# Two attention layers, one core: output projection with tokens on partitions, softmax sums turned to columns through DRAM

## Chip, cores and metric

The kernel runs on one core of a Trainium2 chip, all in float32. The metric is the device time of one execution in microseconds, the median of the runs. The engines carry these names in the profile: PE is TensorE's matmul, PEld its weight load, DVE is VectorE, ACT is ScalarE, POOL is GpSimd, SP is SyncE, which issues the DMAs.

## What is computed

x has 8 images of 32x32 tokens with 256 channels, so 8 batches of N = 1024 tokens. Layer 0 is attention with 4 heads and a residual; layer 1 is attention with a 32-wide key, a gamma and a residual.

```python
# layer 0, per batch; C = 256, h = 4 heads
qkv = xf @ W_qkv                       # 1024 x (4 * 768)
atten = softmax(q k^T * C**-0.5)       # over keys, per head
res = concat_heads(atten @ v) @ W_out + b_out + xf
# layer 1, per batch
f, g, hh = x @ Wf + bf, x @ Wg + bg, x @ Wh + bh
y = gamma * (softmax(g f^T) @ hh) + x
```

## The kernel before

Everything is one pass over *steps*. A step is one head (or layer 1) of one batch and one block (blk) of 512 queries. For each batch the order is the four heads of layer 0, two blocks each, and then layer 1 of the batch before, two blocks; after the last batch its own layer 1 follows. In each step the loop at L801 collects lists of small tasks: the scores of this step, the block sums and the product p x of the step before (`one`), the division and projection of the step before that (`two`), and whatever prepares the next head or batch. Each list comes with a begin and an end between 0 and 1, and `weave` (L755) sorts all tasks by their place in it and issues them in that order. TensorE, VectorE and ScalarE then work through exactly this order[...] (a manual schedule, L771); the order on POOL and SP is left to a scheduler. So the numbers in the lists decide what stands between two dependent tasks.

The weights of a head are folded: W_q W_k^T for the scores and W_v W_out for the output, so a head multiplies p with x itself and then with the folded 256x256 matrix wvo. Large products use seven block products instead of eight (`seven`, L219). It makes three tasks, one, two and three, which collect in three PSUM banks x, y and z: after task one ScalarE copies bank x to e and VectorE adds bank y to it (u); after task two VectorE makes v = y + e and one output block; task three adds two further products into banks y and z, which VectorE must have read by then, and two more output blocks follow. Within one `seven` TensorE thus waits for VectorE between task two and task three, and for ScalarE's e between one and two, unless other work stands there. The six "ps" banks serve these and layer 1's scores; two "psm" banks serve transposes (px, pt), projections (po, pr_v, pm_fg) and the like.

A layer 0 step: `scores` runs two `seven` groups of tokens (g = 0 and 2), each followed by exponentials on ScalarE (L472, L473), which give p. `sums` (L490) makes four block sums s1 to s4 of p for the next `seven`, then the softmax sums: m, rs, and an all-reduce over partitions on POOL, which leaves the sum of every query on all partitions (rb, L524). `invert` (L530) takes a 512-wide reciprocal and stores one row to the tile `check`. `products` (L536) makes y = x^T p with one `seven`. One step later `divide` (L557) multiplies y, 128x1024, with the inverse sums, and `project` (L563) multiplies wvo with y (po, channels on partitions) and adds it into x1T, the transposed output of layer 0. `queries` (L425) makes the next head's q with another `seven`, and its block sums qs. `value_sums` and `key_sums` make block sums of x and of its transpose x0T (from `transpose_rows`, px).

A layer 1 step: `scores` (L649) makes eight 128x512 tiles ps_l, four at a time[...]; ScalarE copies each to s_l, VectorE takes maxima (L702, L706, L708: smax), POOL all-reduces them to cmax (L710), and VectorE subtracts (L717) before ScalarE's exponentials (L722). `values` gives v_l (pr_v), `row_products` (L728) multiplies with it (pa_l), divides by the sum and adds to the rows of x1. Those rows come from `turn_back` (L605), which transposes x1T back. At the end the inverse sums in `check` are tested against limits (L859 to L866); a general branch behind `tc.If` takes over if any lies outside, which these inputs don't do.

## Time and profile before

| what | us |
|---|---|
| median of 3 runs | 2469.9 (2469.7 to 2473.68) |
| the profiled execution's own time | 2468.4 |
| its span | 2466.5 |
| PE busy | 2394.2 |
| DVE busy | 1843.4 |
| ACT busy | 612.8 |
| POOL busy | 249.6 |
| 512-wide reciprocals (L532), 64 | 214.0 |
| divisions of y (L559), 64 | 77.9 |
| additions of po into x1T (L581, L586), 128 | 89.4 |
| all-reduces of the sums (L524), 64 | 213.2 |

A busy time is the time in which at least one instruction of that engine ran, and the span is that of one execution. Matmuls are pipelined, and the page models their ends, so a PE that is 97% busy isn't at its peak 97% of the time. Rows in the timeline read: start, length, engine, line, operation, output<-input, shape, how many, and in brackets how long the engine stood idle before, and what ended that. A row of float32 matmul counts two records for each matmul that the program issues.

### The profile page before, as it was taken

To read this page: it belongs to the slowest core of one execution; us is meant where nothing else is said; L and a number is where in the kernel's file an instruction comes from. 1 tells how busy PE (TensorE), PEld (TensorE's weight loads), DVE (VectorE), ACT (ScalarE), POOL (GpSimd) and SP (SyncE) were. 2 spreads that over 40 slices of the span, in tenths; PEclk is the share of its full clock that TensorE was granted. 3 is DMA by queue.
4 is the path that set the end of the run, shared out by engine and by line. 5 is a ranking of instruction groups with operands and counts; after the bars stand their busy time and mean duration, and the time that the engine had idled before them with its cause. 6 is when DMAs were issued, how large, how long until landed. Compare 5 with 4: busy or idle time off the path is not lost.

```text
span 2466.5 us, 24718 instructions
## 1 busy us (share of the span) xinstructions
PE 2394.2 (97%) x10096; PEld 1858.4 (75%) x10096; DVE 1843.4 (75%) x2398; ACT 612.8 (25%) x985; POOL 249.6 (10%) x93
## 2 busy tenths in 40 slices
PE   8999999999999999999999999999899999999997
PEld 6777777777777677776877768777687776877766
DVE  5778887785878768787687776777767777677764
ACT  2222222232222322223222232222322223222232
POOL 0111111110111101111011110111101111011110
PEclk9999999999999999999999999999999999999999
DMA  3000000000000000000000000000000000000000
GB/s 111 1 1 1 18 1 1 0 1 35 1 1 1 1 35 1 0 1 0 35 1 1 1 0 35 1 1 1 1 35 0 1 1 1 18 1 1 1 9 28
DMA packets 11786, 23.30 MB, mean 9 GB/s; under 512 B 4496, under 2 KB 6416, under 8 KB 11664
## 3 DMA queue, kind: packets, MB, share of 16 engines
q1 hardware_dynamic: 11664, 21.64, 2.5%
q8 instruction: 81, 1.33, 0.2%
q14 instruction: 41, 0.34, 0.0%
HBM read 13.11 MB, written 8.39 MB: 9 GB/s over the span
## 4 chain that ended last, share of the span: by engine, by line
PE 88%; DVE 10%; ACT 1%; issue 1%; DMA 0%; SPq 0%; POOL 0%; DVEq 0%; ACTq 0%
PE psy_y L232 13%; PE psy L232 13%; PE pa_l L735 9%; PE psz L232 9%; PE psz_y L232 9%; PE psx_y L232 9%; PE psx L232 8%; PE po L572 6%; PE psy_q L232 3%; DVE s L511 3%; PE psz_q L232 2%; PE psx_q L232 2%; PE pr_v_l L403 1%; PE ps_l L659 1%; PE pm_fg L383 1%; ACT s_l L668 1%
## 5 line engine op out<-in xcount | busy, mean ns | idle before, releaser
L524 POOL PARTITION_ALL_REDUCE rb<-rs x64 | 213.2, 3332 | 1532.6 <-DVE rs L522 1532.6
L472 ACT ACTIVATE p<-p 128x1024 f32<-128x1024 f32 x128 | 135.3, 1057 | 782.6 <-DVE p L249 782.6
L232 PE MATMUL psy<-qs,xs 128*128 128x256 f32 x1024 | 262.9, 379 | 1.7 <-DVE qs L443 1.7
L232 PE MATMUL psx<-q,x0T 128*128 128x256 f32 x1024 | 262.8, 379 | 0.0
L232 PE MATMUL psz<-q,xs 128*128 128x256 f32 x1024 | 262.8, 379 | 0.0
L572 PE MATMUL po<-y,wvo 128*128 128x512 f32 x512 | 246.3, 604 | 16.4 <-DVE x0T L167 13.0
L232 PE MATMUL psx_y<-p,x 128*128 128x256 f32 x1024 | 241.9, 379 | 0.0
L232 PE MATMUL psz_y<-ss,x 128*128 128x256 f32 x1024 | 241.9, 379 | 0.0
L232 PE MATMUL psy_y<-s,xt 128*128 128x256 f32 x1024 | 241.9, 379 | 0.0
L232 PEld LDWEIGHTS psx<-q,x0T 128*128 128x128 f32 x1024 | 194.2, 190 | 50.2 <-issue 26.8
L735 PE MATMUL pa_l<-v_l,s_l 128*128 128x257 f32 x1024 | 228.3, 380 | 0.1
L735 PEld LDWEIGHTS pa_l<-v_l,s_l 128*128 128x128 f32 x1024 | 194.3, 190 | 32.2 <-issue 3.9
L232 PEld LDWEIGHTS psy<-qs,xs 128*128 128x128 f32 x1024 | 194.5, 190 | 28.5 <-DVE qs L443 2.1
L232 PEld LDWEIGHTS psz<-q,xs 128*128 128x128 f32 x1024 | 194.6, 190 | 26.5
L232 PEld LDWEIGHTS psy_y<-s,xt 128*128 128x128 f32 x1024 | 194.6, 190 | 26.5
L232 PEld LDWEIGHTS psz_y<-ss,x 128*128 128x128 f32 x1024 | 194.6, 190 | 26.5
L232 PEld LDWEIGHTS psx_y<-p,x 128*128 128x128 f32 x1024 | 194.6, 190 | 26.5
L532 DVE RECIPROCAL rb<-rb 128x512 f32<-128x512 f32 x64 | 214.0, 3343 | 0.0
L572 PEld LDWEIGHTS po<-y,wvo 128*128 128x128 f32 x512 | 97.0, 192 | 107.1 <-issue 75.9
L249 DVE TENSOR_TENSOR u<-psy,e 128x512 f32<-128x512 f32 x128 | 88.5, 691 | 105.5 <-PE psy L232 95.8
L261 ACT ACTIVATE p<-psx 128x512 f32<-128x512 f32 x128 | 76.5, 597 | 282.9 <-PE psx L232 282.7
L232 PE MATMUL psy<-qs,x0T 128*128 128x256 f32 x512 | 133.9, 384 | 5.5 <-DVE v L249 5.5
(112 smaller groups left out, 3063.3 us busy)
## 6 DMA issues: line engine op xcount, KB each, us to landing
out_dram<-x SPq DMA_DIRECT2D x15, 512.0 KB, 2.6
x<-in_x_dram SPq DMA_DIRECT2D x14, 512.0 KB, 4.4
w<-in_L_conv_W_qkv_dram SPq DMA_DIRECT2D x4, 768.0 KB, 9.1
x<-in_x_dram SPq DMA_DIRECT2D x4, 256.0 KB, 4.0
w<-in_L_conv_W_out_dram SPq DMA_DIRECT2D x4, 256.0 KB, 9.3
check<-rb SPq DMA_DIRECT2D x64, 2.0 KB, 1.6
out_dram<-x SPq DMA_DIRECT2D x4, 128.0 KB, 1.8
wh_sb<-in_L_conv_Wh_dram SPq DMA_DIRECT2D x1, 256.0 KB, 2.7
```

Of the source, the lines that this page charges most:

```text
L232: nc.tensor.matmul(banks[k][:, ts(i, w)], lhsT=lhsT, rhs=rhs, start=first and n == 0, stop=True, skip_group_check=True,)
L249: nc.vector.tensor_tensor(dst, shaped(banks[k]), shaped(other), ALU.add)
L261: copy(outs["11"](), shaped(banks["x"]))
L383: nc.tensor.matmul(pm[:m], lhsT=w()[:, c, d * P : d * P + m], rhs=src()[:, c, ts(k, NB)], start=(c == 0), stop=(c == CC - 1),)
L403: nc.tensor.matmul(pm[:, ts(j, C)], lhsT=src()[:, c, ts(2 * t2 + j, P)], rhs=w()[:, c, :], start=(c == 0), stop=(c == CC - 1),)
L472: exp(both, both)
L511: made["l"][i]()
L524: nc.gpsimd.partition_all_reduce(t, r.rearrange("p e i -> p (e i)"), P, bass_isa.ReduceOp.add)
L532: nc.vector.reciprocal(r, r)
L572: nc.tensor.matmul(pm, lhsT=folded[self.h][1][:, c, ts(e, P)], rhs=self.y[blk][:, c, :], start=(c == 0), stop=(c == CC - 1),)
L659: nc.tensor.matmul(pm, lhsT=self.f[ts(r, CK), ts(j0 + r, P)], rhs=self.g[ts(r, CK), ts(blk, NB)], start=True, stop=True,)
L735: nc.tensor.matmul(pm[:, : C + 1], lhsT=p[:, j, ts(ti, P)], rhs=v[:, j, : C + 1], start=(j == 0), stop=(j == NT - 1),)
```

## The change

The projection changes sides: y is now the stationary operand, so po has tokens on partitions, and its rows are added straight to the rows of x1. The inverse sum of a query is then one number per partition, and VectorE scales and adds in one operation. To bring the sums from a row to columns, the first row of rb is stored to DRAM and loaded back as a 128x4 tile, and the reciprocal is taken of that tile. Division, x1T's additions and `turn_back` go; x1's rows begin as x + b_out (`residual`), and x1T is made by `transpose_rows` in block 0 of the next batch's head 3. All copies of transposes are on ScalarE. The lists move: block sums s1, s2 at 0.08 to 0.32 of a step, s3, s4 at 0.4 to 0.7, the softmax sums at 0.7 to 0.95, po at 0.4 to 0.8. The test of the inverse sums moves ahead of the last row products. Several pools change size.

```diff
+    bout_sb = const.tile([P, C], F32, tag="bout", name="bout_sb")
+    inverse = const.tile([P, B * HEADS * NBLK * HT], F32, tag="inverse", name="inverse")
...
     def transpose_rows(b, src, dst, layer):
...
-            copy_on(c, dst[b][:, c, ts(k, NB)], pt)
+            nc.scalar.copy(dst[b][:, c, ts(k, NB)], pt)
...
+    def residual(b):
+        def piece(i):
+            if i == 0:
+                rows1[b] = tile_of("rows", [P, NT, C], f"x1_{b}")
+            nc.vector.tensor_tensor(
+                rows1[b][:, ts(i, 2), :], rows[b][:, ts(i, 2), :],
+                bout_sb.unsqueeze(1).broadcast_to([P, 2, C]), ALU.add,
+            )
+        return [partial(piece, i) for i in range(NT // 2)]
...
                 nc.gpsimd.partition_all_reduce(
                     t, r.rearrange("p e i -> p (e i)"), P, bass_isa.ReduceOp.add
                 )
-            return [partial(piece, i) for i in range(4)] + [first, second]
+                line = tile_of("line", [1, NB], f"line_{n}")
+                nc.sync.dma_start(line, t[0:1, :])
+                self.r[blk] = st = tile_of("st", [P, HT], f"st_{n}")
+                with nc.allow_non_contiguous_dma(reason="a row of sums turns into columns"):
+                    nc.sync.dma_start(st, line.rearrange("o (t p) -> p (o t)", p=P))
+            return [partial(piece, i) for i in range(4)], [first, second]
...
         def invert(self, blk):
-            r = self.r[blk]
-            nc.vector.reciprocal(r, r)
-            k = (self.b * HEADS + self.h) * NBLK + blk
-            nc.sync.dma_start(check[k : k + 1, :], r[0:1, :])
+            n = self.first + blk * HT
+            nc.vector.reciprocal(inverse[:, n : n + HT], self.r[blk])
...
-        def divide(self, blk):
...
         def project(self, blk):
+            def task(t2):
+                pm = tile_of("psm", [P, NB], f"po_{self.name}_{blk}_{t2}")
+                for j in range(2):
+                    for c in range(CC):
+                        nc.tensor.matmul(
+                            pm[:, ts(j, C)],
+                            lhsT=self.y[blk][:, c, ts(2 * t2 + j, P)],
+                            rhs=folded[self.h][1][:, c, :],
+                            start=(c == 0),
+                            stop=(c == CC - 1),
+                        )
+                for j in range(2):
+                    ti = 2 * t2 + j
+                    n = self.first + blk * HT + ti
+                    acc = rows1[b][:, blk * HT + ti, :]
+                    nc.vector.scalar_tensor_tensor(
+                        acc, pm[:, ts(j, C)], inverse[:, n : n + 1], acc, ALU.mult, ALU.add
+                    )
...
-        def turn_back(self):
...
-        s=2, rows=2, xT=3, v=2, q=2, qs=2, xt=1, ss=1, s2=1, s3=1, m0=1, m1=1, rs=1, rb=2,
-        y=1, e=2, u=2, w=2, eh=2, uh=2, wh=2, r=8, ps=6, psm=2,
+        s=2, rows=4, xT=2, v=2, q=2, qs=2, xt=1, ss=1, s2=1, s3=1, m0=1, rs=1, rb=1,
+        y=2, e=2, u=2, w=1, eh=1, uh=1, st=2, r=8, line=4, ps=6, psm=2,
...
-            if a.h == 1 and blk == 0 and a.b + 1 < B:
+            if a.h == 2 and blk == 0 and a.b + 1 < B:
                 load_x(a.b + 1)
+            if a.h == 0 and blk == 1:
+                lists.append((residual(a.b), 0.3, 1))
...
-            lists.append((u.sums(k), 0.08, 0.4))
-            lists.append(([partial(u.invert, k)], 0.6, 0.7))
-            lists.append((u.products(k), 0.42, 1.0))
+            sums, keys = u.sums(k)
+            lists.append((sums[:2], 0.08, 0.32))
+            lists.append((sums[2:], 0.4, 0.7))
+            lists.append((keys, 0.7, 0.95))
+            lists.append((u.products(k), 0.4, 1.0))
...
-            lists.append(([partial(u.divide, k)], 0, 0.04))
-            lists.append((u.project(k), 0.05, 0.4))
+            lists.append(([partial(u.invert, k)], 0.34, 0.36))
+            lists.append((u.project(k), 0.4, 0.8))
...
-        if change and blk == 1 and a.b > 0:
-            lists.append((nxt[0].queries(), 0.05, 0.4))
+        if change and a.b > 0:
+            if blk == 0:
+                lists.append((transpose_rows(a.b - 1, rows1, x1T_of, 1), 0.02, 0.4))
+            else:
+                lists.append((nxt[0].queries(), 0.05, 0.4))
...
-        if not l0 and blk == 1:
-            lists.append((a.turn_back(), 0, 0.25))
-            if nxt is None:
-                lists.append((final.queries(), 0.45, 1))
+        if nxt is None:
+            lists.append((transpose_rows(B - 1, rows1, x1T_of, 1), 0.82, 0.9))
+            lists.append((final.queries(), 0.9, 1))
...
-    run(own[:1], s0[:1], prod[:1], s0[1:], own[1:2], prod[1:2])
-    weave((own[2:] + prod[2:] + back, 0, 1), (s1, 0, 1), (p0, 0, 1))
-    weave((final.products(0), 0, 1), (p1, 0, 1))
+    run(own[:1], s0[:1], prod[:1], s0[1:], prod[1:2])
+    weave((prod[2:] + own[1:], 0, 1), (s1, 0.3, 0.9), (p0, 0.1, 1))
+    weave((final.products(0), 0, 1), (p1, 0, 0.9), ([judge, decide], 0.9, 1))
```

## The prediction

> **What bounds the kernel now.** I read first the page's busy times and its chain of work that ended last, then the busy times by stretch, then the timeline of single stretches, and beside them the order in which the changed kernel's instructions stand on each engine.

> ```profile
> PE 2394.2 (97%) x10096; PEld 1858.4 (75%) x10096; DVE 1843.4 (75%) x2398; ACT 612.8 (25%) x985; POOL 249.6 (10%) x93
> ...
> PE 88%; DVE 10%; ACT 1%; issue 1%; DMA 0%; SPq 0%; POOL 0%; DVEq 0%; ACTq 0%
> ```

> TensorE sets the end. A 256-column matmul record starts every 0.2155 us when nothing holds it (64 of 257 columns took 13.87 us in the chain, 0.217 each). With that price for every record I come to about 2351 us of work and some 115 us in which TensorE stands or runs slowly: about 18 in the first 60 us, 25 in the last 130, the rest at places that repeat in each batch. VectorE matters only where TensorE waits for it.

> ```profile
> 1121.00:1154.00 33.00, 29.56 (x131) 21.43 (x130) 28.59 (x34) 10.29 (x17) 6.82 (x2) 0.95 0.00 1
> 1154.00:1185.00 31.00, 30.00 (x118) 18.97 (x117) 18.74 (x26) 10.80 (x18) 1.78 (x1) 0.94 0.00 1
> ...
> 1246.00:1307.00 61.00, 60.73 (x252) 47.52 (x251) 48.30 (x60) 12.49 (x23) 6.47 (x2) 1.00 0.00 1
> ```

> Columns: stretch, length, PE, PEld, DVE, ACT, POOL, granted clock. The first two are the two layer 1 steps of a batch, the third two layer 0 steps. Layer 0 has nearly no gap (0.3 in 61 us), layer 1 has several us, and there the clock falls too. So removing VectorE work from layer 0 can save next to nothing; what counts is what stands between two dependent TensorE groups.

> [...]

> **The change, part by part.**

> Vector work. Removed per layer 0 step: the 512-wide reciprocal (L532, 3.343 us), the division (L559, 1.217), two additions x1T<-po (L586, 2 x 0.683): 5.93. Added: four 128x256 multiply-adds from PSUM at 0.484 (row L745), a 4-wide reciprocal at about 0.17 (row L743): 2.11. Eight times, four residual pieces of 0.69. Over 64 steps 244 us less and 22 more. The cover is total: this time lies beside TensorE, so I book it at nothing; if it were on the path it would be most of 222.

> TensorE. po: 8 records of 512 columns become 16 of 256, the same columns; weight loads take 190 ns under 215. The transposes of x1 are as many as before (128 records). Zero. They move from the second layer 1 step to head 3, block 0: +2.1 us there, -2.1 there.

> DMAs. One row store to check (1.6) becomes a row store and a column load of 512 elements, both on SP's queue, behind the all-reduce (3.3). The column load is not in the trace: not below zero, as it replaces nothing; at least 1.6, and at most 9 (the 256-element bout_sb load landed after 9.2, behind weights). I take 2.5. The sums end about 0.5 us before the next step starts, so columns stand about 7.5 us into it; VectorE's reciprocal comes at 7 to 8 there, its next consumer for TensorE some 4 us later. Nothing for 1.6 to 6; 9 would cost about 2 us in 24 steps. Queued behind that reciprocal on VectorE are two additions into p and the third block sum; behind the row store on SP's queue stand the column load, x loads and stores of out, none needed within 10 us. On POOL the all-reduce moves to the step's end, ahead of the next maximum's; rb has one buffer now, free once the row has landed, 10 us before that maximum. All at nothing, with that cover; without it each us late counts once per step.

> *Layer 0, the lost spacer.* This is the main item. A scores group is three tasks; the third overwrites a bank that VectorE must first read (tile v). Before, po stood between:

> ```profile
> 1250.26 1.03 PE L232 MATMUL psy<-qs,xs 128*128 128x256 f32 x4
> ...
> 1251.12 1.88 PE L572 MATMUL po<-y,wvo 128*128 128x512 f32 x4
> ...
> 1253.27 1.13 PE L232 MATMUL psy<-qs,x0T 128*128 128x256 f32 x4 [0.27 <-DVE v L249]
> ```

> po is moved to 0.4-0.8 of the step, so in block 0 of heads 1 and 2 the first group runs one, two, three with nothing between. The trace has that case at the start:

> ```profile
> 21.23 1.02 PE L232 MATMUL psy_q<-xs,wt 128*128 128x512 f32 x2
> ...
> 22.29 0.69 DVE L249 TENSOR_TENSOR v_q<-psy_q,e_q 128x512 f32<-128x512 f32 x1 [1.81 <-PE psy_q L232]
> ...
> 23.04 1.13 PE L232 MATMUL psy_q<-x0T,wt 128*128 128x512 f32 x2 [0.78 <-DVE v_q L249]
> ```

> 1.81 us from start to start, less 0.86 of work: 0.95, with 0.1 of restart 1.05.

> Second, the block sums' last adds go to 0.7-0.95. In a step with the next head's query sums, VectorE then has, after v (ready 5.0 us before the step's end): v 0.72, p 0.61, m 1.14, qs 0.61, rs 0.72 and 0.35, qs 0.61, two y at 0.38: 5.5 us, before the last two adds into p. Those come 1.2 us later than now (1244.42, which is 0.67 before the next step's first matmul). The exponentials follow, then the copy e:

> ```profile
> 1244.42 0.69 DVE L249 TENSOR_TENSOR p<-psy,e 128x512 f32<-128x512 f32 x1 [0.44 <-PE psy L232]
> ...
> 1245.09 1.03 PE L232 MATMUL psx<-q,x0T 128*128 128x256 f32 x4
> ...
> 1245.15 1.06 ACT L472 ACTIVATE p<-p 128x1024 f32<-128x1024 f32 x1 [5.31 <-DVE p L249]
> ...
> 1246.63 0.57 ACT L255 COPY e<-psx 128x512 f32<-128x512 f32 x1
> ```

> e ends 2.1 after the step's start now, 3.3 then; task two may start at 2.6, so TensorE stalls 0.77 + 0.1 (after head 0, with one residual piece more, 0.6 longer). Per batch: head 1 2.55, head 2 1.92, head 3 0.35 (transposes fill): 4.8. Times eight, and 1.9 once more in batch 1's head 0: 40.5. The present layer 0 waits (v L249 and v_q, with restarts) are 14.2 and go. Net **+26**.

> *Layer 1.* Step one: all four px copies now on ScalarE, 0.6 each between copies of ps_l (2.05 for four). Walked from px: second ps_l copies end at 7.3, maxima and smax 3.1, s2 at 10.5 to 11.7; psy_y needs s2 and TensorE is there at 8.8: a stall of 2.9, and 1.3 among the px; VectorE's backlog then leaves 0.5 at the next psx_q. Before, po waits of 0.9 and 2.3 and the px and pr_v waits made 5.9. Step two loses pt and po as fillers:

> ```profile
> 1167.95 0.59 ACT L668 COPY s_l<-ps_l 128x512 f32<-128x512 f32 x1 [0.23 <-PE ps_l L659]
> 1168.57 1.23 DVE L702 TENSOR_TENSOR m_l<-s_l 128x1024 f32<-128x1024 f32 x1 [4.21 <-ACT s_l L668]
> ...
> 1171.70 0.68 DVE L249 TENSOR_TENSOR v_q<-psy_q,e_q 128x512 f32<-128x512 f32 x1
> ```

> From the last copy's end to v_q's 3.84 us; TensorE has only 1.7 of query work meanwhile, so it stalls 2.95 (1.05 or covered today), and 1.8 at the ps_l banks as now. Both steps: 61.3 and the moved 2.1, against 63.6 today: -0.2.[...] Between 0 and 2.95; I take +1.6 net, six times: **+10**.

> *The end.* The last layer 1 and the final pass: 29.4 and 81.9 by the same walk, against 32.4 and 89.0 today: the final turn-back, 3.8 + 1.0 + 1.5 of waits, is gone. -10.1[...]. The test of the sums (flag at 2460.9) no longer follows the last row (2458.5): -2.4. Net **-12**. The start: 0, within 1.

> Sum: +26 +10 -12 = +24. The profiled execution took 2468.4 (span 2466.5), the median is 2469.9, 1.5 above: 2492 for a profile, **2494** predicted.

> **Rivals.**
> (a) *VectorE's relief wins*, faster: every layer 1 wait that VectorE ended shrinks, as 3.8 us per step less stand before s2 and v_q. For it: 28.6 of 33 busy there. Against it: the waits hang on ScalarE's copies and on order, which the relief doesn't touch. If both stalls fell to about 1: -4 six times, -12 at the end, and +4 in layer 0: 2438. It decides once s2 follows TensorE by under 1 us.
> (b) *The late adds don't bite*: the exponentials are in time, only the 17 bare gaps of 1.05 stay (+4), layer 1 +10, end -12: 2472, no change.
> (c) *The columns come late*: at 15 us instead of 7.5, VectorE stalls some 7, TensorE 3, in 32 steps: about 2590. Nothing in the trace speaks for such a DMA on an idle queue.

> **Numbers.** Forecast 0.74, (a) 0.10, (b) 0.11, (c) 0.05. Own range of the forecast 2483[...] to 2507[...]. For 8 in 10 it reaches down to (b) and takes in the few us of a slow column DMA: 2470 to 2510. Faster or slower counts from 0.2%, 5 us, about what a measurement here can tell from none: faster 0.10, same 0.11, slower 0.79.

> **What would show it.** PE waits for ACT e and DVE v in block 0 of heads 1 and 2, near 0.8 and 0.95; psy_y waiting for s2, psy_q for v_q, near 2.9; no wait of VectorE for the column DMA; DVE near 1610 busy (1843 - 244 + 22 and 11 of x0T copies that go to ScalarE). I am wrong if TensorE has no gap at those places, or a batch takes under 304 us (now 302.6).

## The result, and the profile after

| kernel | median | runs | against before, 95% interval |
|---|---|---|---|
| before | 2470.5 us | 2469.7 to 2473.7 | |
| after | 2511.8 us | 2508.6 to 2518.5 | 1.0168 (1.0145 to 1.0191) |

Slower by 41, where the forecast said 24. The profiled execution of after took 2508.6 (span 2506.8), that of before 2468.4 (2466.5): 40.2 to explain, in which the forecast had 24.

The page of after, busy times and the chain of work that ended last:

```profile
PE 2411.3 (96%) x10608; PEld 1965.0 (78%) x10608; DVE 1580.1 (63%) x2477; ACT 617.6 (25%) x1001; POOL 250.7 (10%) x93
...
PE 80%; DVE 14%; ACT 5%; issue 1%; DMA 0%; SPq 0%; DVEq 0%; ACTq 0%
```

VectorE lost 263 us of work, 30 more than reckoned (1610 was forecast), and yet its share of the chain rose from 10% to 14%, and ScalarE's from 1% to 5%. Less work on an engine, more waiting for it: the order has become the trouble. TensorE's own waits in after (who waited, for whom: us in total, times, longest; the profile counts idle time, about 0.17 less than the forecast, which counts from start to start less the work between):

```profile
PE psx L235 <- ACT e L258: 24.1, 17, 2.5
PE psy_y L235 <- DVE s L528: 19.2, 7, 3.0
PE psy L235 <- DVE v L252: 13.7, 18, 0.8
PE psy_q L235 <- DVE v_q L252: 12.4, 7, 2.7
```

These are the four waits that the forecast named, each at its place. The second and third have the size forecast, the fourth is smaller (1.8 on average, 2.7 at most, for 2.95); the first has a longest wait of 2.5, 2.6 from start to start, where 1.4 was forecast.

I cut both executions at the first TensorE instruction of each layer 1 pair of steps (px) and at the first psx of head 0 behind it. Worked out from the start times in the two traces:

| stretch | before | after | change, all of them |
|---|---|---|---|
| start to the first layer 1 (two batches of layer 0) | 519.2 | 534.3 | +15.1 |
| layer 1's two steps, six times | 63.6 to 64.2 | 61.4 or 63.1 | -9.7 |
| the rest of a batch's layer 0, six times | 239.0 | 246.5 to 246.8 | +45.8 |
| last layer 1 to the end | 130.4 | 119.3 | -11.1 |

Of the +7.65 in each layer 0 stretch 2.1 is x1's transposes, which only moved there from layer 1. What is left, 5.5, is more than the forecast's 4.8 less 1.8 = 3.0. Layer 1 and the end are as forecast or better. So the miss is in layer 0, and there in one place. The timeline of after where head 0 ends and head 1 begins in one batch:

```profile
960.36 0.43 DVE L539 TENSOR_TENSOR rs<-rs 128x256 f32<-128x256 f32 x1
...
960.96 3.53 POOL L541 PARTITION_ALL_REDUCE rb<-rs  x1 [30.97 <-DVE rs L539]
961.31 0.42 DVE L252 TENSOR_TENSOR y<-psy_y,e_y 128x256 f32<-128x256 f32 x1
...
961.64 0.41 DVE L252 TENSOR_TENSOR y<-psz_y,u_y 128x256 f32<-128x256 f32 x1
961.97 2.06 DVE L384 TENSOR_TENSOR x<-x,bout_sb 128x512 f32<-128x512 f32 x1
...
963.96 0.68 DVE L252 TENSOR_TENSOR p<-psy,e 128x512 f32<-128x512 f32 x1
...
964.67 1.06 ACT L489 ACTIVATE p<-p 128x1024 f32<-128x1024 f32 x1 [8.36 <-DVE p L252]
...
966.15 0.56 ACT L258 COPY e<-psx 128x512 f32<-128x512 f32 x1
...
966.77 1.66 PE L235 MATMUL psx<-q,x0T 128*128 128x256 f32 x4 [2.47 <-ACT e L258]
...
968.23 1.91 PE L235 MATMUL psy<-qs,xs 128*128 128x256 f32 x4
...
970.93 1.13 PE L235 MATMUL psy<-qs,x0T 128*128 128x256 f32 x4 [0.78 <-DVE v L252]
```

Read it from the last line back. TensorE waits 2.47 for e, e stands behind two exponentials on ScalarE, these wait for p, p stands behind the fourth residual piece x on VectorE, and that piece took 2.06 instead of the 0.68 of its three siblings. It is the one of the four that runs beside POOL's all-reduce. Then the four psx take 1.66 and the four psy 1.91 instead of 1.03: from 968.20 to 970.20 the granted clock is 0.50 (last section). Two things, then, that the forecast had not put in this place: the piece's 1.38, and a slow clock in every batch. The experiments take them apart.

### The profile page after: what moved, and what is told of

Same layout as the page of the kernel before. It is cut to its first block, busy times and chain, and to the rows that moved or that the text cites. A ratio compares the mean times of both kernels' runs of the same rounds, so it can differ in the third digit from the quotient of the medians.

```text
span 2506.8 us, 26004 instructions
## 1 busy us (share of the span) xinstructions
PE 2411.3 (96%) x10608; PEld 1965.0 (78%) x10608; DVE 1580.1 (63%) x2477; ACT 617.6 (25%) x1001; POOL 250.7 (10%) x93
## 4 chain that ended last, share of the span: by engine, by line
PE 80%; DVE 14%; ACT 5%; issue 1%; DMA 0%; SPq 0%; DVEq 0%; ACTq 0%
PE psy L235 12%; PE psy_y L235 11%; PE pa_l L726 9%; PE psx L235 8%; PE po L585 8%; PE psx_y L235 8%; PE psz L235 7%; PE psz_y L235 6%; PE psy_q L235 3%; PE psz_q L235 2%; PE psx_q L235 2%; DVE m L533 2%; DVE p L252 2%; ACT s_l L659 1%; DVE v L252 1%; ACT p L489 1%
## 5 line engine op out<-in xcount | busy, mean ns | idle before, releaser
L235 PE MATMUL psx<-q,x0T 128*128 128x256 f32 x1024 | 270.6, 387 | 24.7 <-ACT e L258 24.1
L235 PE MATMUL psy<-qs,xs 128*128 128x256 f32 x1024 | 269.2, 386 | 1.7 <-DVE qs L460 1.7
L235 PE MATMUL psy_y<-s,xt 128*128 128x256 f32 x1024 | 247.4, 385 | 19.2 <-DVE s L528 19.2
L585 PE MATMUL po<-wvo,y 128*128 128x256 f32 x1024 | 241.9, 379 | 0.0
L596 DVE SCALAR_TENSOR_TENSOR x<-po,inverse,x 128x256 f32<-128x256 f32 x256 | 112.0, 479 | 205.3 <-PE po L585 205.3
L585 PEld LDWEIGHTS po<-wvo,y 128*128 128x128 f32 x1024 | 194.6, 190 | 26.5
L258 ACT COPY e<-psx 128x512 f32<-128x512 f32 x128 | 74.0, 578 | 305.4 <-PE psx L235 305.4
L235 PE MATMUL psy<-qs,x0T 128*128 128x256 f32 x512 | 134.0, 384 | 13.7 <-DVE v L252 13.7
L252 DVE TENSOR_TENSOR v<-psy,e 128x512 f32<-128x512 f32 x128 | 88.5, 692 | 86.9 <-PE psy L235 86.7
```

Of the source, the lines that this page charges most:

```text
L235: nc.tensor.matmul(banks[k][:, ts(i, w)], lhsT=lhsT, rhs=rhs, start=first and n == 0, stop=True, skip_group_check=True,)
L252: nc.vector.tensor_tensor(dst, shaped(banks[k]), shaped(other), ALU.add)
L258: nc.scalar.copy(scratch("e"), banks["x"])
L585: nc.tensor.matmul(pm[:, ts(j, C)], lhsT=self.y[blk][:, c, ts(2 * t2 + j, P)], rhs=folded[self.h][1][:, c, :], start=(c == 0), stop=(c == ...
L596: nc.vector.scalar_tensor_tensor(acc, pm[:, ts(j, C)], inverse[:, n : n + 1], acc, ALU.mult, ALU.add)
```

## The experiments

Most change a line or two in the lists of after's steps; e8 and e9 change before, c1 to c3 combine. "After" is 2511.8, "before" the median of its runs on the same chip, 2468.6 to 2471.4.

**The residual piece: contention or queue?**

```diff
-                lists.append((residual(a.b), 0.3, 1))
+                lists.append((residual(a.b), 0.3, 0.9))    # e1
+                lists.append((residual(a.b), 0.1, 0.7))    # e2
```

> Only the fourth residual piece of head 0's second step moves: it stands ahead of the last two additions of the block sums instead of behind them, so it runs before the all-reduce and not beside it; the VectorE work ahead of the step's last additions into p is the same. Theory (contention): in the profile of after this piece takes 2.06 us beside the all-reduce and the other three 0.68, and that 1.38 is the part of the 2.6 us wait for e that the forecast lacked. Then the piece takes 0.69, the wait for e after head 0 falls from 2.5 to about 1.1, and the time by 8 x 1.38 = 11, to 2501; by some 14 more, to 2487, if the slow clock that follows this wait in every batch (1.7 us each) goes too. Rival (length of VectorE's queue alone): the wait stays at 2.5 and the time at 2511.

> All four residual pieces stand ahead of the step's last v, where VectorE has idle time. Theory: the wait for e after head 0 becomes that after head 2 (0.65), 8 x 1.9 = 15 less, and with stalls of 0.65 and 0.95 the slow clock goes as it did not appear after head 2: 8 x 1.7 = 14 less: 2483. Rival (the slow clock hangs on the bare group, not on the length of the wait for e): it stays in every batch, 2497. Under the queue-length rival of the other run this one gives most of the gain and the other none.

Measured: e1 2489.5 us (2487.7 to 2494.5), 1.0088 of before (1.0071 to 1.0105); e2 2482.1 (2479.4 to 2484.4), 1.0050 (1.0034 to 1.0067). The same place in e1's timeline:

```profile
951.19 0.68 DVE L384 TENSOR_TENSOR x<-x,bout_sb 128x512 f32<-128x512 f32 x1
...
953.10 3.52 POOL L541 PARTITION_ALL_REDUCE rb<-rs  x1 [31.57 <-DVE rs L539]
...
954.72 0.68 DVE L252 TENSOR_TENSOR p<-psz,u 128x512 f32<-128x512 f32 x1
...
956.31 0.56 ACT L258 COPY e<-psx 128x512 f32<-128x512 f32 x1
...
956.93 1.13 PE L235 MATMUL psx<-q,x0T 128*128 128x256 f32 x4 [1.07 <-ACT e L258]
...
957.90 1.03 PE L235 MATMUL psy<-qs,xs 128*128 128x256 f32 x4
```

The piece is still on VectorE's queue ahead of p, but it takes 0.68, the wait for e is 1.07, and the four psy behind it take 1.03 again. That holds in all eight batches; the mean granted clock is 0.995, for 0.990 in after. A layer 0 stretch falls from 246.6 to 243.8: of 2.83, 1.38 is the piece, and the other 1.45 fits the clock (in e4 below, a stretch without the slow clock takes 245.2, the others, with it, 246.5 to 246.9). The rival, that the length of VectorE's queue alone made the wait, falls: the queue was as long. In e2 the wait for e after head 0 is 0.5, and a stretch is 243.2.

**The lost spacer.** First its place, then what it was worth in the kernel before:

```diff
-            lists.append((u.project(k), 0.4, 0.8))
+            po = u.project(k)                              # block 0 of heads 1, 2:
+            lists.append((po[:1], 0.16, 0.18))             # e3, with invert at 0.14
+            lists.append((po[:1], 0.38, 0.4))              # e5
+            lists.append((po[1:], 0.6, 0.8))
```

> In block 0 of heads 1 and 2 the first po and its inverse return to the first group, between tasks two and three; everything else of after stays, the late sums too. Theory (the lost spacer costs 0.95 + 0.1 in each of 16 steps): waits of TensorE for v fall from 18 us to about 4, the waits for e stay, 2495; 2481 if the slow clock goes with them. Rival (columns too late for this place): VectorE's reciprocal waits for the column DMA, over 0.5 us each, and the additions into p behind it come later: 2505 or more.

> The spacer again, now at its right place: a step has six tasks of scores, so in block 0 of heads 1 and 2 the first po must stand past 0.25 and before 0.42 to come between tasks two and three (in the run before it fell between one and two, where its multiply-add went ahead of v). Only that po moves. Theory (the lost spacer is 0.95 + 0.1 in 16 steps): waits for v fall from 18 to about 4, waits for e stay at 28: 2511 - 17 = 2494; 2481 if the slow clock goes with them. Rival (the wait for e alone sets the slow clock): it stays in every batch, 2494 or a little above.

Measured: e3 2505.9 (2501.6 to 2512.0), e5 2500.3 (2497.3 to 2503.1), 1.0115 of before (1.0098 to 1.0132). In e5 the waits for v in the 16 groups are gone, those for e stand at 24.1 as in after, and a layer 0 stretch falls from 246.6 to 244.6, two groups of 1.05: the price of the spacer holds. The time fell by 11.5 and not by 17, since in layer 1 the slow clock came in all pairs here (62.7 to 66.0; mean granted clock 0.988) and in after in half of them (61.4 or 63.1; 0.990). Behind the wait for e it stayed in six of eight batches, mostly as the rival has it.

In e3, 1.0158 of before (1.0140 to 1.0176), po fell between tasks one and two, where I had not meant it. It then covers part of the wait for e (longest 0.7), but its multiply-adds go ahead of v on VectorE, and v comes later by more. e3 shows something else: here VectorE asks for the columns early, and waits for them. Its timeline behind head 2's start:

```profile
1023.06 0.36 SPq L548 DMA_DIRECT2D st<-line  x1
...
1025.30 0.18 DVE L554 RECIPROCAL inverse<-st 128x4 f32<-128x4 f32 x1 [1.35 <-DMA st<-line]
...
1025.59 0.87 DVE L596 SCALAR_TENSOR_TENSOR x<-po,inverse,x 128x256 f32<-128x256 f32 x2
...
1026.38 0.68 DVE L252 TENSOR_TENSOR v<-psy,e 128x512 f32<-128x512 f32 x1
...
1027.11 1.13 PE L235 MATMUL psy<-qs,x0T 128*128 128x256 f32 x4 [1.98 <-DVE v L252]
```

A wait of 1.35 for the DMA puts v and the psy behind it off by as much; at head 2's start it comes in all eight batches (1.2 to 1.35), at head 1's in none. In after the load is issued at 965.65 and lands 2.1 later, and the reciprocal comes at 972.64:

```profile
965.65 0.38 SPq L548 DMA_DIRECT2D st<-line  x1
...
972.64 0.17 DVE L554 RECIPROCAL inverse<-st 128x4 f32<-128x4 f32 x1
```

The time between landing and reciprocal is 5 us in the median of the 64 steps and 0.2 at the least, and in none did VectorE wait: the forecast's third rival (columns late) never had its condition. With the reciprocal at 0.15 of a step instead of 0.35 that cover is gone.

```diff
-            lists.append((u.project(k), 0.05, 0.4))
+            bare = l0 and blk == 0 and a.h in (1, 2)
+            lists.append((u.project(k), *((0.4, 0.8) if bare else (0.05, 0.4))))    # e8, on before
```

> The kernel before, with both po of block 0 in heads 1 and 2 moved from 0.05-0.4 to 0.4-0.8 of the step, and nothing else of the change. Theory: 16 bare groups of 0.95 + 0.1, the waits for e stay hidden because the sums are early: + 17, 1.007 times before. Rival (the fuller VectorE of this kernel makes v or p late at their new place): + 25 or more. Rival (a po there was no spacer, the wait for v has another cause): within 3 us of before.

Measured: 2530.3 (2529.1 to 2531.6), 1.0236 of before (1.0219 to 1.0253): +59, three times the theory, and beyond the rival. Its timeline at head 1's start:

```profile
964.87 1.22 DVE L559 TENSOR_TENSOR y<-y,rb 128x1024 f32<-128x1024 f32 x1
...
966.81 1.22 DVE L511 TENSOR_TENSOR ss<-p 128x1024 f32<-128x1024 f32 x1
...
968.06 1.23 DVE L511 TENSOR_TENSOR s<-ss,p 128x1024 f32<-128x1024 f32 x1
969.20 1.22 DVE L511 TENSOR_TENSOR s<-p 128x1024 f32<-128x1024 f32 x1
970.34 0.68 DVE L249 TENSOR_TENSOR v<-psy,e 128x512 f32<-128x512 f32 x1
...
971.08 1.40 PE L232 MATMUL psy<-qs,x0T 128*128 128x256 f32 x4 [2.54 <-DVE v L249]
```

v is not late by its own length, it stands behind three block sums. The two po's of before hid 2.7 us there from start to start, not 0.95, and 16 such waits with the slow clock behind 15 of them (mean granted clock 0.984, for 0.994 in before) make the 59. So the change's two moves seem to belong together: with po gone from there, spreading the block sums (in after one, at 967.36, stands ahead of v) brings the bare group to 0.95. No run takes the spreading alone out of after.

**The late sums.**

```diff
-            lists.append((keys, 0.7, 0.95))
+            lists.append((keys, *((0.62, 0.74) if l0 else (0.7, 0.95))))    # e7
```

> The block sums' last additions go from 0.7-0.95 to 0.62-0.74 of a layer 0 step, ahead of the last group's v instead of between v and the last additions into p; the residual pieces stay, so now the third of them falls beside the all-reduce. Theory (the late additions are what TensorE's waits for e come from): the waits for e after heads 0, 1 and 2 nearly vanish (28 us and 6 of restarts and slow issue), the slow clock after them too (8 x 1.7): 2511 - 34 to - 45, 2466 to 2477. Rival (VectorE's work is only pushed ahead of v): v comes 2 to 3 us later and TensorE waits for it at the step's end, half comes back: about 2490.

Measured: 2470.4 (2468.4 to 2473.3), 0.9996 of before (0.9987 to 1.0005). This one line gives back all that the change cost. The lines of e7 at the same place:

```profile
942.37 3.53 POOL L541 PARTITION_ALL_REDUCE rb<-rs  x1 [26.97 <-DVE rs L539]
...
944.05 1.40 DVE L460 TENSOR_TENSOR qs<-q 128x512 f32<-128x512 f32 x1
...
946.76 0.68 DVE L384 TENSOR_TENSOR x<-x,bout_sb 128x512 f32<-128x512 f32 x1
...
950.18 1.13 PE L235 MATMUL psx<-q,x0T 128*128 128x256 f32 x4 [0.46 <-ACT e L258]
```

The waits for e fall from 24.1 to 3.7, the waits for v stay at 13.7, no slow clock follows a head's start (mean granted clock 0.994), and the fourth piece, now after the all-reduce's end, takes 0.68. Beside the all-reduce stands qs now, at 1.40 here and 1.70 elsewhere, where TensorE doesn't wait for it. The rival's late v does not show: the products of psy_y and psz_y stand between tasks two and three, and in these lines' batch v ends 1.8 us before task three starts.

**Layer 1.**

```diff
-            lists.append((sums[:2], 0.08, 0.32))
+            lists.append((sums[:2], 0.08, 0.32 if l0 else 0.24))                        # e4
-            lists.append((queries, 0.07, 0.39))
+            lists.append((queries, *((0.07, 0.39) if l0 else (0.05, 0.32))))            # e6
```

> In layer 1's first step only, the second block sum stands on VectorE ahead of the second maximum instead of behind three maxima. Theory (order on VectorE, not its load, makes psy_y wait): psy_y no longer waits for s2 (19 us in seven steps), and part of the slow clock of that step goes (4.7): 2487 to 2493. Rival (VectorE is full there): the maxima come 1.2 us later and the wait reappears at the query products or at the value rows' banks, half comes back: about 2502.

> In layer 1's second step only, task two of the next head's query product stands ahead of the second group of ps_l, so that v_q stands ahead of the second maxima on VectorE. Theory (v_q waits behind maxima that wait for ScalarE's copies): the wait for v_q (15 us in seven steps) falls to about 2 and the wait of ps_l for a bank (1.1 each) shrinks: 2511 - 15 = 2496. Rival (the wait moves to psx_q, whose e_q stands behind four copies of ps_l on ScalarE, or to ps_l): under 5 us, 2507.

Measured: e4 2494.8 (2492.8 to 2495.1), 1.0103 (1.0086 to 1.0120); e6 2488.1 (2484.8 to 2489.7), 1.0063 (1.0046 to 1.0079). In e4 psy_y's wait of 19.2 is gone; 5.1 come back where pr_v waits for the multiply-adds that free its bank, the rival's place but a quarter of the wait, not half. In e6 the wait for v_q falls from 12.4 to 0.8, that of ps_l for a bank from 4.0 to under 0.8, and a pair of steps takes 58.8 instead of 61.4 or 63.1. Both waits were VectorE's order, maxima that wait for ScalarE standing ahead of what TensorE needs. The slow clock of layer 0 stays in six batches of e4 and five of e6 (mean granted clock 0.990 in both), so a part of both gains is the other two and three.

**Is VectorE's work worth time?**

```diff
-            r = self.r[blk]
-            nc.vector.reciprocal(r, r)
-            k = (self.b * HEADS + self.h) * NBLK + blk
-            nc.sync.dma_start(check[k : k + 1, :], r[0:1, :])
+            pass
...
-            lists.append(([partial(u.divide, k)], 0, 0.04))    # e9, on before
```

> The kernel before without the 512-wide reciprocal, without the division of y and without the row that it stores for the test of the sums: the scaling by inverse sums is left out, TensorE's work is the same, VectorE has 64 x 4.56 = 292 us less. Theory (this VectorE work is covered): only the po that waits for the divided y in layer 1 gains (6.5 us in seven waits), 2471 - 5 to - 10: 2461 to 2466. Rival (VectorE's relief is worth most of its length where layer 1 waits): - 25 or more, under 2446.

The kernel is left without the scaling by the inverse sums. Measured: 2468.3 (2466.4 to 2469.6), 0.9991 of before (0.9982 to 1.0000). The first line of e9's page:

```profile
PE 2394.3 (97%) x10096; PEld 1864.9 (76%) x10096; DVE 1570.1 (64%) x2270; ACT 612.5 (25%) x985; POOL 249.0 (10%) x93
```

VectorE is busy 273 us less (1843.4 to 1570.1), and the median falls by 1.8, less even than the theory's 5. The 3.3 of idle time in which po waited for the division in layer 1 are gone, and px waits 2.2 more there for an addition to x1T (2.5 for 0.3). The first rival of the forecast, that VectorE's relief wins, has no ground: in before's order there is next to nothing in it to win.

**Together.** c1 has the edits of e4, e5, e6 and e7; c2 also e2's; c3 is c1 with this:

```diff
-            nc.scalar.copy(dst[b][:, c, ts(k, NB)], pt)
+            (nc.vector.tensor_copy if vector and k == 0 else nc.scalar.copy)(dst[b][:, c, ts(k, NB)], pt)
...
-            lists.append((transpose_rows(b, rows, xT_of, 0), 0.02, 0.35))
+            turned = transpose_rows(b, rows, xT_of, 0, not l0)    # layer 1: vector
+            lists.append((turned[:2], *((0, 0.08) if not l0 else (0.02, 0.185))))
+            lists.append((turned[2:], *((0.14, 0.35) if not l0 else (0.185, 0.35))))
```

> Four of the moves together on the changed kernel: the sums' last additions ahead of the last v, the first po between tasks two and three in block 0 of heads 1 and 2, the second block sum ahead of the second maximum and the query product's task two ahead of the second group of ps_l. Theory (each removes its own wait): 2470 with the first alone, - 17 for the bare groups, - 17 and - 20 for the two of layer 1: 2416 to 2425. Rival (they share VectorE's free time, so that gains overlap): about 2440.

> As c1, with the residual pieces at 0.1-0.7 of head 0's second step as well. Theory: with the sums already ahead of v the pieces no longer meet a full VectorE there; what is left after head 0 (0.6 in eight steps) goes: 0 to 5 less than c1. Rival (they now delay v, which stands behind sums and pieces): up to 10 more than c1.

> As c1, and in layer 1's first step the first two of the four px are copied by VectorE, which is idle there for 3.3 us, ahead of the first ps_l. Theory: ScalarE's copies of ps_l come 1.1 earlier in six steps, and waits of px and ps_l (some 15 us in all) halve: 5 to 8 less than c1. Rival (the copies push the first maximum and the block sums later on VectorE): no gain.

Measured: c1 2408.3 (2405.6 to 2408.6), 0.9746 of before (0.9730 to 0.9763); c2 2401.8 (2401.4 to 2402.6), **0.9724** (0.9708 to 0.9740); c3 2408.2 (2406.6 to 2409.8), 0.9752 (0.9735 to 0.9768). c1 and c2 beat both kernels. c1 is 8 below the range that I had added up from single runs: with no repeated stall over 0.7 of idle time left, no slow clock comes between the start and the last 2 us (mean granted clock 1.00). c2 gains 6 more, a little over the theory's 5. c3's edit brings nothing: px's 2.1 of waits for ScalarE go, but pr_v's wait for VectorE grows from 5.1 to 8.0, and a pair of layer 1's steps takes 55.1 for 55.0. The page of c2, and its longest waits of TensorE:

```profile
PE 2372.0 (99%) x10608; PEld 1957.9 (82%) x10608; DVE 1600.8 (67%) x2477; ACT 617.8 (26%) x1001; POOL 236.9 (10%) x93
...
PE 92%; DVE 4%; ACT 2%; issue 1%; POOL 1%; DMA 0%; SPq 0%; DVEq 0%; ACTq 0%
```

```profile
PE pr_v_l L419 <- DVE x L596: 5.1, 7, 1.3
PE px L339 <- DMA x<-in_x_dram: 3.7, 2, 3.5
PE px L339 <- ACT x0T L342: 2.0, 6, 0.3
```

VectorE is busier than in after and its share of the chain is 4% instead of 14%. What TensorE still waits for is above all the banks of pr_v and the start's loads.

## Why the forecast was right, and where it was wrong

*That it gets slower, and by which waits:* right. From start to start, as the forecast counts, the wait for v in the bare groups is 0.95 (forecast 0.95), the wait for e at head 2's start 0.65 (0.77), at head 3's 0.23 (0.25), psy_y's for s2 2.85 (2.9). VectorE's relief counts for next to nothing (e9: 273 us of it, 1.8 in the median), and no step waits for the columns.

*Layer 1, +10:* too high. At full clock (granted 1.00) a pair of steps takes 61.4, and 61.3 was walked; with the slow clock (0.95) 63.1. It came in three of six pairs, and there in both steps, but only step one's cost time, 1.7: step two's fell ahead of the wait for v_q, which shrank from 2.7 to 1.1. So 1.7 in half the pairs; the forecast's step from the walked -0.2 to +1.6, in every pair, was an estimate of mine. With the moved 2.1 that is -1.6 + 2.1 = +0.5, six times +3, so 7 less. (For v_q's wait the forecast shows 3.84 and 1.7, which leave 2.1 and not its 2.95; the missing part isn't shown.)

*The end, -12:* right, -11.1.

*Layer 0, +26: the step that failed.* In "head 1 2.55" the wait for e after head 0 stood at 1.4 + 0.1, "with one residual piece more, 0.6 longer". The piece was priced at the 0.69 of a piece alone (0.6 of it as added wait). Beside the all-reduce it took 2.06, and the change puts exactly this piece there, because it moves the sums, and with them the all-reduce, to the step's end. The sum lacked 1.38 x 8 = 11. This was to be seen in the trace of before: there qs, also an addition of two tiles in SBUF, had stood beside the all-reduce all along, at 1.77 instead of 0.68 in 25 of 64 cases, while an addition that reads PSUM beside it took its 0.68:

```profile
1230.74 3.23 POOL L524 PARTITION_ALL_REDUCE rb<-rs  x1 [17.51 <-DVE rs L522]
1231.17 0.68 DVE L249 TENSOR_TENSOR p<-psz,u 128x512 f32<-128x512 f32 x1
...
1231.76 1.77 DVE L443 TENSOR_TENSOR qs<-q 128x512 f32<-128x512 f32 x1
```

I priced the piece by its kind of operation and did not ask why qs has 1105 ns on average in its row where its sibling q has 682.

The second lack follows from the first. The half clock followed the idle time of 2.47 in all eight batches, that of 1.07 in none (e1): 1.45 x 8 = 11.6 more. The forecast's sum had no slow clock in layer 0, and in layer 1 only as an estimate. Together 22.6, less 7 in layer 1, plus 1 at the end: 16.6, which is 2508.6 - 2492 of the profiled execution. That it fits so well is partly luck: in the table layer 0 is up by 60.9, of which seven moved sets of transposes are 14.7, so 46 for the forecast's 26. That is 20 and not 22.6, as other waits there were shorter than forecast, and the seventh set's 2.1, which the sum seems to take out of the end and to add nowhere, stands against it. The median of after lies 3.2 above its profiled execution, which had the highest granted clock of its four runs (0.990, the others 0.986 to 0.988); that of before lies 1.5 to 2.1 above.

*The range* ended at 2510 because its upper end was built of my estimates of slow stretches and of a slow column DMA. Nothing in it stood for an operation that grows beside another engine.

*The rivals:* (b), that the late additions don't bite, falls with e7: their place was worth 41 us, with what it brought along.

Open: no run moves a stall alone, or changes the operands of an addition alone. That the moment of a stall of 2.5 decides whether the slow clock follows, and that two operands in SBUF make an addition wait beside the all-reduce, is read from the traces together (last section): 48 stalls and 347 additions.

## What to carry to other kernels

When an edit moves an operation of GpSimd, list what VectorE will now run beside it, and price those operations from rows that already stood beside it (qs in before: 1.77), not from their mean (1.105); in the last section the price depends on when they begin. An operation that comes "off the path" on a busy engine still has a place in a queue: here 273 us less of VectorE's work gave 1.8 us and one line of order gave 41. Add up stalls by place and not only in total: the one of 2.6 cost its length and 1.45 of slow clock in each batch of after; those of 0.95 cost their length (e5).

## What the runs showed of the hardware

The 14 traces agree on which VectorE operations an all-reduce holds up. Of those that ran wholly beside one, more than 2300 with an operand in PSUM kept their time (in after, 187 beside all-reduces of the sums took 0.41 to 0.69), and so did 101 reciprocals of one SBUF tile (0.17). But all 241 additions of two SBUF tiles (37 of them in before and after) that began more than 1.13 us before the end of an all-reduce of the sums took longer than alone, and each ended 0.44 or 0.45 before that end, whenever it had begun: the piece, 1.0 after the all-reduce, took 2.06, qs 1.40 to 1.85, the block sums of x0T, late in one of 4.1, as little as 0.71. The 106 that began later took their 0.68 or 0.69. That the longer ones waited until about 1.13 before the recorded end, and then took their 0.68, fits all of them; the wait itself has no record in the trace, nor has what the all-reduce does in its last part, and spans on GpSimd are rough.

The all-reduce is longer too: in after it takes 3.52 to 3.61 in the 25 cases in which an addition of two SBUF tiles still ran when it began, 3.23 in the other 39.

The experiments agree with this in layer 0. Idle times of 2.46 to 2.54 stand at 48 places there (after, e4, e5, e6, e8), and the half clock followed at 40, each with 2.01 us or more in one interval; the other eight were divided, with 1.98 at most. In e4, where the half clock first begins at 92.2, an edge lies 75 intervals later at 348.2, and the wait that ended at 349.27 was cut into 1.4 and 1.1: no slow clock in that batch. Of the stalls of 1.84 to 1.98 at head 2's start in e3, the half clock followed three of eight, with 1.86 to 1.94 in one interval, where the interval with 1.90 in after had none behind it, so the border isn't sharp; of those of 1.53 at head 1's start it followed none. The half clock first begins 529.99 us after the start of the span in before and 93.42 in after, which is 127.9 intervals apart and no whole number, so which batches are slow is in part chance. In layer 0 the half clock lasted 3.41 in after, and twice that at some places of e4 and e6 (a layer 0 stretch in e6 takes 245.2 without it, 248.1 with twice 3.41).

The granted clock by stretch in after, with and without such a stall (start and end, length, PE, PEld, DVE, ACT, POOL, clock, then the DMA engines' share and GB/s):

```profile
964.50:995.00 30.50, 27.44 (x120) 23.36 (x121) 17.67 (x29) 6.57 (x11) 1.68 (x1) 0.94 0.01 1
995.00:1026.00 31.00, 31.00 (x131) 24.68 (x130) 19.25 (x30) 6.67 (x12) 1.56 (x1) 1.00 0.01 1
```

A load of 512 single elements from a row to columns landed 2.1 us after its issue in the median (3.4 at most), 0.5 more than the 2 KB row store that it replaces took in before (1.6).
